# One TensorE step and one reciprocal for the denominators of a global and a 3x3 local softmax

## The chip, the cores and the metric

The kernel runs on one core of a Trainium2 chip, all in float32, in one launch. The metric is the device time of that launch in microseconds (us), the median of three executions.

## What is computed

The input is x, 4 images of 64x64 pixels with 256 channels. Two layers follow one another. Layer 0 is full self-attention over the 4096 pixels of an image. Layer 1 is a depthwise 3x3 convolution to 768 channels, a two-layer perceptron, and attention in a 3x3 window. Cut to what matters:

```
# layer 0
energy = einsum('bnd,bmd->bnm', q, k)                 # q, k: 32 channels
attn   = softmax(energy, axis=-1)                     # over 4096 pixels
x      = gamma * einsum('bnm,bmc->bnc', attn, v) + x
# layer 1
perceived = depthwise_conv3x3(x)                      # 3 outputs per channel
h  = x + w_up2 @ gelu(w_up1 @ perceived + b_up1) + b_up2
q, k, v = split(h @ w_qkv.T + b_qkv)
w  = softmax over the 9 neighbours of (q . k_neighbour / 16)
out = h + sum_i w_i * v_neighbour_i
```

So there are two softmaxes, and each needs a denominator per pixel: the sum of the exponentials.

## The kernel before

**Layout.** Channels or keys lie on the 128 partitions, pixels along the free axis. One *slot* is a block of 512 pixels (8 image rows); 4 images of 8 blocks make 32 slots, numbered 0 to 31. The kernel writes each engine's instruction order out by hand: the order of the Python calls is the order in which each engine runs its instructions.

**The global attention of one slot** walks over its 4096 keys in 16 *points* of 256 keys. `energy` (L262) makes 512 keys' scores with four matmuls of 32 rows each, in a tile `e` that takes four PSUM banks and has one buffer. `weight` (L274) is ScalarE's exponential from `e` into a tile `p` (three buffers, 256 keys each); it runs two points ahead of `product` (L279), which multiplies `p` with the values into the two accumulators `acc`. `add_up` (L293) adds the `p` tiles on VectorE into `den`, 128 partial sums per pixel, one on each partition.

**The denominators.** `finish` (L305), at the end of a slot, multiplies `den` with a 128x128 matrix of ones (`dps`, L310), which sums over the partitions and leaves the same sum on all 128; VectorE takes the reciprocal (`rden`, L312), scales the two accumulators (`o`, L316) and adds them to the image in SBUF (L320). The local attention does the same five slots behind (`LAG_ATT`): `local_sum` (L601, mostly GpSimd) makes `lsum`, again 128 partial sums per pixel, at point 12 of a slot, and `local_denominator` (L629), at point 1 of the next slot, multiplies it with ones (`ld`, L631) and takes a reciprocal (`lrden`, L633). `local_product` (L636) multiplies by it at points 3 and 5.

**The other work of a slot** is laid on the points by the list `jobs` (L701): `hidden` (L380, the perceptron's first layer, four parts of 6 matmuls, each followed by ScalarE's Gelu), `update` (second layer), `guide`, `scores`, `local_values`. Each takes a PSUM bank by `job_bank`; in the slots these and `dps` share two banks with the tag "m", taken in turn. After the last slot comes a *tail* (L774 on), in which the banks go round over "m", "e" and "acc", and VectorE still has much convolution (`perceive`, L366) to do.

**The next image.** During the last slot of an image (slots 7, 15 and 23; each of them is the slot with `nxt`, L711) the queries, keys and values of the next image's eight blocks are projected. `fetch` (L166) brings each block of x with two DMAs from the SyncE queue into a tile `xc` (two buffers). The first two, for the blocks 8 and 9 say, are issued ahead of point 0 (L714); `project_qk` (L195), which works on both blocks, follows at the end of point 1. A tile that takes over a buffer is written only when the last reader of the tile before it, in program order, is done, wherever in the program that reader stands.

Of the kernel before, what the change touches and what calls it, by code (L numbers as in the profile page):

```python
# [15 lines left out]
P = 128  # L16
# [3 lines left out]
CH = C // P  # L20
HP, WP = H + 2, W + 2
NB = 512
# [21 lines left out]
LAG_PERC, LAG_HID, LAG_ATT = 2, 3, 5  # L44
# [3 lines left out]
def attention_then_perception_kernel(  # L48
# [19 lines left out]
    nc = tc.nc  # L68
# [8 lines left out]
    ones = const.tile([P, P], F32, tag="ones", name="ones")  # L77
# [5 lines left out]
    def unshifted():  # L83
# [4 lines left out]
        def tile_of(shape, tag, name, bufs=1):  # L88
            return pool.tile(shape, F32, tag=tag, name=name, bufs=bufs)

        def bank(tag, name):
            return psum.tile([P, NB], F32, tag=tag, name=name, bufs=2)
# [5 lines left out]
        def job_bank(name):  # L98
            turns.append(turns.pop(0))
            if turns[-1] == "e":  # L100
                return psum.tile([P, GRP, NB], F32, tag="e", name=name, bufs=1)[:, 0, :]
            return bank(turns[-1], name)
# [7 lines left out]
        def renew(slot, cs=slice(0, CH)):  # L110
            b, g = divmod(slot, NBLK)
            at = slice((1 + g * RB) * WP, (1 + (g + 1) * RB) * WP)
            nc.sync.dma_start(out=xp[:, cs, at], in_=x[b, :, cs, at])
# [44 lines left out]
        def watch(values):  # L158

            nc.gpsimd.tensor_tensor(watched, watched, values, ALU.add)  # L160
# [85 lines left out]
        def projections(s):  # L246
            pair = [lambda: project_qk(s)] if s % 2 == 0 else []
            return pair + [lambda: project_v(s, 0), lambda: project_v(s, 1)]
# [8 lines left out]
                )  # L257


        energies, weights, sums, accs = {}, {}, {}, {}  # L260

        def energy(s, G):  # L262

# [41 lines left out]
        def finish(s):  # L305
            g = s % NBLK
            den = sums.pop(s)

            dps = bank("m", f"dps_{s}")
            nc.tensor.matmul(dps, lhsT=ones, rhs=den[:, 0, :], start=True, stop=True)  # L310
            rden = tile_of([P, NB], "rden", f"rden_{s}", 2)
            nc.vector.reciprocal(rden, dps)  # L312
            os = []
            for c, acc in enumerate(accs.pop(s)):
                o = tile_of([P, NB], "o", f"o_{s}_{c}", 3)
                nc.vector.scalar_tensor_tensor(o, acc, gam[:, 0:1], rden, ALU.mult, ALU.mult)  # L316
                os.append(o)
            for c, o in enumerate(os):
                dst = xv[:, c, 1 + g * RB : 1 + (g + 1) * RB, 1 : 1 + W]
                nc.vector.tensor_tensor(  # L320
                    dst, o.rearrange("p (h w) -> p h w", w=W), dst, ALU.add
                )
            watch(den[:, 0, :])
            watch(rden)
            for o in os:
                watch(o)


        percs, hids, hs = {}, {}, {}
# [95 lines left out]

        guides, lvs, near_ws, lsums, lrdens, pads, spares, results = [], {}, {}, {}, {}, {}, {}, {}
        wg = pool.tile([P, CH, C], F32, tag="wg", name="wg")
        small = pool.tile([P, 2 * CH + 1], F32, tag="small", name="small")  # L430
        bg, wc, bc = small[:, :CH], small[:, CH : 2 * CH], small[0:1, 2 * CH :]
# [194 lines left out]
            watch(t)  # L626
            lsums[s] = t

        def local_denominator(s):  # L629
            ps = job_bank(f"ld_{s}")  # L630
            nc.tensor.matmul(ps, lhsT=ones, rhs=lsums.pop(s), start=True, stop=True)  # L631
            lrdens[s] = tile_of([P, NB], "rden", f"lrden_{s}", 2)
            nc.vector.reciprocal(lrdens[s], ps)  # L633
            watch(lrdens[s])
# [26 lines left out]
        def job(f, s, *args, n=NSLOT):  # L661
            return [lambda: f(s, *args)] if 0 <= s < n else []
# [32 lines left out]
        for slot in range(NSLOT):  # L695
            b, g = divmod(slot, NBLK)
            if b > 0:
                renew(slot)
            k, a = slot - LAG_HID, slot - LAG_ATT

            jobs = [  # L701
                job(hidden, k, 0), job(hidden, k, 1) + job(local_denominator, a),
                job(hidden, k, 2), job(local_product, a, 0), job(hidden, k, 3),
                job(local_product, a, 1), job(update, k, 0), job(update, k, 1), [],
                job(guide, k, 0), job(guide, k, 1), job(scores, k, 0),
                job(scores, k, 1) + job(local_sum, k - 1), job(local_values, k, 0),
                job(local_values, k, 1), [],
            ]
            if slot in (1, 2):
                jobs[0] = [lambda: next(combine)] * 2  # L710
            nxt = []  # L711
            if g == NBLK - 1 and b + 1 < B:
                nxt = [projections(slot + 1 + i) for i in range(NBLK)]
                for i in range(2):  # L714
                    fetch(slot + 1 + i)
            if slot == 0:
                nxt = [early_jobs[2 * i : 2 * i + 2] for i in range(NG)]
            conv = perceive(slot - LAG_PERC, whole) if slot >= LAG_PERC else iter(())
            n_steps, stepped = NPC * (TAPS - 1), 0
            extra = iter(())  # L720
            if slot == NSLOT - 1:

                extra = perceive(slot - 1, [(i, 0, RB - 1) for i in range(NPC // 2)])
            for point in range(points):
                G, half = divmod(point, 2)
                after = slot + (G + 1) // NG, (G + 1) % NG
                if half == 0:
                    if G == NG // 2 and slot + 1 < NSLOT:
                        spread_queries(slot + 1)

                    if G == NG // 2:
                        for do in job(border, k - 1):
                            do()
                    if after[0] < NSLOT:
                        energy(*after)
                if after[0] < NSLOT:
                    weight(*after, half)
                for do in jobs[point]:
                    do()
                product(slot, G, half)  # L740

                if point == 0:
                    add_up(slot, 0, 0)
                if point < points - 1:
                    add_up(slot, *divmod(point + 1, 2))

                while stepped < min(n_steps, -(-(point + 1) * n_steps // (points - 2))):
                    next(conv, None)
                    stepped += 1
                    if stepped % 2:  # L750
                        next(extra, None)
                if slot == 0 and point == NG:

                    next(combine)
                    blqk = loaded(b_lqk, "blqk")
                    wperc = loaded(w_perc, "wperc")
                    bperc = loaded(b_perc, "bperc")
                    wup1 = loaded(w_up1, "wup1")
                    bup1 = loaded(b_up1, "bup1")
                    wup2 = loaded(w_up2, "wup2")  # L760
                    bup2 = loaded(b_up2, "bup2")
                    nc.sync.dma_start(out=wlv, in_=w_qkv[:, :, 2 * C :])
                    blv = loaded(b_lv.partition_broadcast(P), "blv", [P, C])
                if nxt and half == 1:
                    for do in nxt[G]:
                        do()
                    if slot and G + 2 < NBLK:
                        fetch(slot + 1 + G + 2)
            for _ in chain(conv, extra):
                pass  # L770
            finish(slot)


# [15 lines left out]
        last = NSLOT - 1  # L789
        for k in range(NSLOT - LAG_HID, NSLOT):  # L790
            a = k - LAG_ATT + LAG_HID
            if k == last:
                for _ in conv:
                    pass
            run(
                (hidden, k, 0, 6), (hidden, k, 1, 6), (local_denominator, a, 0),
                (hidden, k, 2, 6), (local_product, a, 0, 1), (hidden, k, 3, 6),
                (local_product, a, 1, 1), (update, k, 0, 3), (update, k, 1, 2),
                (local_values, k, 0, 1), (guide, k, 0, 1), (local_values, k, 1, 1),
                (guide, k, 1, 1),  # L800
            )
            if k == last:
                below(NSLOT)
                local_values(NSLOT, 0)
            run((scores, k, 0, 1), (scores, k, 1, 1), (border, k - 1, 0), (local_sum, k - 1, 0))
        guide(NSLOT, 0)
        run(
            (scores, NSLOT, 0, 0), (scores, NSLOT, 1, 0), (border, last, 0),
            (local_denominator, last - 1, 0), (local_sum, last, 0),
            (local_product, last - 1, 0, 0), (local_product, last - 1, 1, 0),  # L810
            (local_denominator, last, 0), (local_product, last, 0, 0), (local_product, last, 1, 0),
        )

        test = [tile_of([P, NB], "o", f"test_{i}", 3) for i in range(2)]
# [405 lines left out]
```

## Time and profile before

| | |
|---|---|
| time, median of 3 | 3648.2 us (3646.78 to 3649.05) |
| span of the profiled execution | 3645.1 us, 29412 instructions |
| TensorE (PE) busy | 3599.6 us, 99% |
| VectorE (DVE) busy | 2448.6 us, 67% |
| ScalarE (ACT) busy | 1176.8 us, 32% |
| GpSimd (POOL) busy | 721.2 us, 20% |
| mean granted TensorE clock | 0.996 of full |
| reciprocals, `rden` and `lrden` | 32 and 32, 107.4 us of VectorE each |

PE is TensorE's matmuls and PEld its weight loads; POOL is GpSimd. One float32 matmul of the program stands as two instructions in the profile, so 2048 products are 4096 records. Records of a run overlap a little: what a matmul takes of TensorE's time is read from the starts of neighbours, not from the duration beside it. In lists of groups, the number after `x` is a count, then come busy time and the mean of one in ns, and after the second bar the idle time of the engine just before the group with the releaser that ended it. In a timeline the columns are start, duration (us), engine, line, operation, count and, in brackets, the idle time before it.

### The profile page before, as it was taken

How to read it: one execution, taken by the hardware profiler on the slowest of the kernel's cores; microseconds unless marked ns; L12 is line 12 of the kernel's file. 1: busy time of each engine (PE TensorE's matmuls, PEld its weight loads, DVE VectorE, ACT ScalarE, POOL GpSimd, SP SyncE). 2: the span in 40 equal slices, each digit the busy share in tenths (PEclk: the TensorE clock that was granted, in tenths of full speed). 3: DMA queues.
4: the chain of work that ended last, by engine and by line, in shares of the span. 5: the costliest groups of instructions: out<-in, count | busy, mean ns of one | idle time of the engine just before them, and what ended most of it. 6: DMA issues, size and time to landing. Idle time of an engine off the chain costs nothing.

```text
span 3645.1 us, 29412 instructions
## 1 busy us (share of the span) xinstructions
PE 3599.6 (99%) x11350; PEld 1706.7 (47%) x11350; DVE 2448.6 (67%) x2727; ACT 1176.8 (32%) x1324; POOL 721.2 (20%) x725
## 2 busy tenths in 40 slices
PE   9999999999999999999999999999999999999987
PEld 4444444454444444455444444444544444444444
DVE  3385676657666767766677667676666776766884
ACT  2233333323333333332333333333333333333321
POOL 1010112111222221121112222211121122222232
PEclk9999999999999999999999999999999999999999
DMA  3000000010000000101000000011100000000000
GB/s 103 6 3 4 0 9 21 18 44 15 15 15 3 12 15 15 27 23 38 15 15 15 15 3 12 15 27 33 28 15 15 15 15 15 4 12 15 6 10 21
DMA packets 84532, 64.68 MB, mean 18 GB/s; under 512 B 57280, under 2 KB 62528, under 8 KB 84256
## 3 DMA queue, kind: packets, MB, share of 16 engines
q1 hardware_dynamic: 83568, 62.19, 6.3%
q8 instruction: 91, 1.49, 0.2%
q10 hardware_dynamic: 816, 0.53, 0.0%
q14 instruction: 57, 0.47, 0.0%
HBM read 41.52 MB, written 18.81 MB: 17 GB/s over the span
## 4 chain that ended last, share of the span: by engine, by line
PE 97%; DVE 2%; issue 0%; ACT 0%; POOL 0%; DMA 0%; SPq 0%; ACTq 0%; DVEq 0%; POOLq 0%
PE acc L287 49%; PE hid L385 18%; PE e L268 7%; PE dx L411 6%; PE lv L537 3%; PE g L496 3%; PE v L234 3%; PE s L573 2%; PE lo L642 2%; DVE perc L366 1%; PE qk L200 1%; PE ld L631 1%; PE dps L310 1%; DVE lrden L633 0%; DVE rden L312 0%; PE c L520 0%
## 5 line engine op out<-in xcount | busy, mean ns | idle before, releaser
L287 PE MATMUL acc<-p,v 128*128 128x512 f32 x4096 | 1842.2, 595 | 0.1
L366 DVE SCALAR_TENSOR_TENSOR perc<-xp,wperc,perc 128x512 f32<-128x512 f32 (+2 forms) x1560 | 1305.9, 840 | 314.7 <-ACT perc L362 280.7
L287 PEld LDWEIGHTS acc<-p,v 128*128 128x128 f32 x4096 | 769.4, 190 | 917.3 <-issue 913.5
L276 ACT ACTIVATE p<-e 128x1024 f32<-128x1024 f32 x512 | 524.4, 1024 | 1516.1 <-PE e L268 904.1
L385 PE MATMUL hid<-perc,wup 128*128 128x512 f32 x1536 | 689.2, 598 | 1.6 <-DVE perc L366 1.6
L301 DVE TENSOR_TENSOR den<-den,p 128x1024 f32<-128x1024 f32 x480 | 597.0, 1244 | 44.3 <-ACT p L276 40.6
L385 PEld LDWEIGHTS hid<-perc,wup 128*128 128x128 f32 x1536 | 284.2, 190 | 391.4 <-issue 384.3
L268 PE MATMUL e<-qa,ka 32*128 32x512 f32 x2048 | 292.0, 640 | 0.0
L160 POOL TENSOR_TENSOR watched<-watched,lo 128x512 f32<-128x512 f32 x64 | 130.4, 2037 | 624.4 <-DVE lo L649 624.1
L411 PE MATMUL dx<-hid,wup 128*128 128x512 f32 x512 | 232.8, 598 | 0.0
L389 ACT ACTIVATE hid<-hid,bup 128x512 f32<-128x512 f32 x128 | 88.0, 687 | 400.3 <-PE hid L385 400.3
L312 DVE RECIPROCAL rden<-dps 128x512 f32<-128x512 f32 x32 | 107.4, 3358 | 160.4 <-PE dps L310 160.4
L592 POOL TENSOR_TENSOR lp<-lp,near 128x396 f32<-128x396 f32 x60 | 58.1, 970 | 739.0 <-ACT lp L588 739.0
L276 ACT ACT_TABLE_LOAD x116 | 148.8, 1283 | 151.2 <-issue 120.1
L549 DVE TENSOR_TENSOR lv<-lv,blv 128x256 f32<-128x256 f32 x130 | 49.2, 420 | 193.2 <-PE lv L537 193.2
L633 DVE RECIPROCAL lrden<-ld 128x512 f32<-128x512 f32 x32 | 107.4, 3357 | 82.3 <-PE ld L631 82.3
L417 DVE SCALAR_TENSOR_TENSOR h<-dx,bup,xp 128x256 f32<-128x256 f32 x128 | 56.0, 480 | 152.1 <-PE dx L411 149.3
L268 PEld LDWEIGHTS e<-qa,ka 32*128 32x128 f32 x2048 | 79.9, 182 | 164.6 <-issue 162.0
L411 PEld LDWEIGHTS dx<-hid,wup 128*128 128x128 f32 x512 | 94.7, 190 | 129.2 <-issue 120.2
L362 ACT ACTIVATE perc<-xp,bperc,wperc 128x512 f32<-128x512 f32 (+2 forms) x195 | 154.6, 796 | 0.0
L389 ACT ACT_TABLE_LOAD x119 | 152.7, 1283 | 2.2
L537 PE MATMUL lv<-wlv,h 128*128 128x256 f32 x520 | 128.6, 390 | 12.3 <-DVE h L417 11.0
(91 smaller groups left out, 2030.9 us busy)
## 6 DMA issues: line engine op xcount, KB each, us to landing
xp<-in_x SPq DMA_DIRECT2D x30, 528.0 KB, 4.1
out<-lo SPq DMA_DIRECT2D x60, 256.0 KB, 2.0
xc<-in_x SPq DMA_DIRECT2D x48, 256.0 KB, 3.8
qa<-packed SPq DMA_DIRECT2D x124, 64.0 KB, 2.1
ka<-st SPq DMA_DIRECT2D x124, 16.0 KB, 1.8
packed<-st SPq DMA_DIRECT2D x31, 64.0 KB, 1.9
wup<-in_w_up SPq DMA_DIRECT2D x1, 1536.0 KB, 7.0
xp<-in_x SPq DMA_DIRECT2D x4, 264.0 KB, 3.9
```

Of the source, the lines that this page charges most:

```text
L160: nc.gpsimd.tensor_tensor(watched, watched, values, ALU.add)
L234: nc.tensor.matmul(ps[:, i * C : (i + 1) * C], lhsT=xc[:, kin, bass.ts(2 * pair + i, P)], rhs=wv[:, kin, :], start=(kin == 0), stop=(kin = ...
L268: nc.tensor.matmul(e[:, j, :], lhsT=key[rows, :], rhs=queries[s][rows, :], start=True, stop=True,)
L276: nc.scalar.activation(p, energies[s, G][:, 2 * half : 2 * half + 2, :], AF.Exp)
L287: nc.tensor.matmul(accs[s][c], lhsT=v[:, 2 * half + i, bass.ts(c, P)], rhs=p[:, i, :], start=(first and i == 0), stop=(G == NG - 1 and hal ...
L301: nc.vector.tensor_tensor(den, den, p, ALU.add)
L362: nc.scalar.activation(acc, win, AF.Identity, bias=bperc[:, half, j : j + 1], scale=wt)
L366: nc.vector.scalar_tensor_tensor(acc, win, wt, acc, ALU.mult, ALU.add)
L385: nc.tensor.matmul(ps, lhsT=wup1[:, i, bass.ts(d, P)], rhs=percs[s][i], start=(i == 0), stop=(i == NPC - 1),)
L389: nc.scalar.activation(hids[s][:, d, :], ps, AF.Gelu, bias=bup1[:, d : d + 1])
L411: nc.tensor.matmul(ps, lhsT=wup2[:, d, bass.ts(c, P)], rhs=hids[s][:, d, :], start=(d == 0), stop=(d == NHC - 1),)
L537: nc.tensor.matmul(ps[:, half * C : (half + 1) * C], lhsT=keys_of(s, t, half, kin), rhs=wlv[:, kin, :], start=(kin == 0), stop=(kin == CH ...
```

## The change

`finish` now sums both denominators at once. The matrix of ones is cut to 64 columns and used twice: once on `den`, with its result on PSUM partitions 0 to 63, and once on `lsum` of the local attention, with its result on partitions 64 to 127 of the same bank. The two matmuls sit on the two column halves of TensorE. One reciprocal then turns both. Since each result lies on one half only, copies bring it to both halves: two on VectorE for the global denominator, within `finish`, and two on ScalarE for the local one, in `local_denominator`, which keeps its place at point 1 of the next slot. The purpose is to save a matmul on TensorE and a reciprocal on VectorE in each slot.

It holds where both exist: in `finish` of slots 4 to 31, which is 28 times. Slots 0 to 3 keep the old form, and so do the last four local denominators, in the tail, under the name `last_denominator`. Three things come with it: the reciprocal goes to a tile `turned`, for which the two buffers `xc` are borrowed; the second part of `hidden` moves from point 1 to point 0, ahead of the slot's first `product`; and the tail calls `job_bank` one time fewer.

```diff
         def finish(s):
             den = sums.pop(s)
             dps = bank("m", f"dps_{s}")
-            nc.tensor.matmul(dps, lhsT=ones, rhs=den[:, 0, :], start=True, stop=True)
             rden = tile_of([P, NB], "rden", f"rden_{s}", 2)
-            nc.vector.reciprocal(rden, dps)
+            a = s - LAG_ATT + 1
+            if a < 0:
+                nc.tensor.matmul(dps, lhsT=ones, rhs=den[:, 0, :], start=True, stop=True)
+                nc.vector.reciprocal(rden, dps)
+            else:
+                for half, weights_ in zip(halves, (den[:, 0, :], lsums.pop(a))):
+                    nc.tensor.matmul(
+                        dps[half], lhsT=ones[:, : P // 2], rhs=weights_, start=True, stop=True
+                    )
+                turned = tile_of([P, CH, NB], "xc", f"turned_{s}", 2)[:, 0, :]
+                nc.vector.reciprocal(turned, dps)
+                for half in halves:
+                    nc.vector.tensor_copy(rden[half], turned[halves[0]])
+                lrdens[a] = turned
...
+        def local_denominator(s):
+            turned, lrdens[s] = lrdens[s], tile_of([P, NB], "rden", f"lrden_{s}", 2)
+            for half in halves:
+                nc.scalar.copy(lrdens[s][half], turned[halves[1]])
+            watch(lrdens[s])
...
-        def local_denominator(s):
+        def last_denominator(s):
...
-                job(hidden, k, 0), job(hidden, k, 1) + job(local_denominator, a),
+                job(hidden, k, 0) + job(hidden, k, 1), job(local_denominator, a),
...
-                (hidden, k, 0, 6), (hidden, k, 1, 6), (local_denominator, a, 0),
+                (hidden, k, 0, 6), (hidden, k, 1, 6),
+                (local_denominator if k < last - 1 else last_denominator, a, 0),
```

More of the change, by code (lines that the diff above doesn't have):

```diff
@@ L257, in spread_queries @@
                 )
-        energies, weights, sums, accs = {}, {}, {}, {}
+        energies, weights, sums, accs, lsums, lrdens = {}, {}, {}, {}, {}, {}
+        halves = slice(0, P // 2), slice(P // 2, P)
         def energy(s, G):
@@ L423, in update @@
                 )
-        guides, lvs, near_ws, lsums, lrdens, pads, spares, results = [], {}, {}, {}, {}, {}, {}, {}
+        guides, lvs, near_ws, pads, spares, results = [], {}, {}, {}, {}, {}
         wg = pool.tile([P, CH, C], F32, tag="wg", name="wg")
@@ L808, in unshifted @@
             (scores, NSLOT, 0, 0), (scores, NSLOT, 1, 0), (border, last, 0),
-            (local_denominator, last - 1, 0), (local_sum, last, 0),
+            (last_denominator, last - 1, 0), (local_sum, last, 0),
             (local_product, last - 1, 0, 0), (local_product, last - 1, 1, 0),
-            (local_denominator, last, 0), (local_product, last, 0, 0), (local_product, last, 1, 0),
+            (last_denominator, last, 0), (local_product, last, 0, 0), (local_product, last, 1, 0),
         )
```

## The prediction

> **What bounds the kernel now.** I read the chain of work that ended last first, because it says whose time is the kernel's time. Its shares by engine:
>
> ```profile
> PE 97%; DVE 2%; issue 0%; ACT 0%; POOL 0%; DMA 0%; SPq 0%; ACTq 0%; DVEq 0%; POOLq 0%
> ```
>
> Then the list of waits, for TensorE alone (total us, times, longest):
>
> ```profile
> PE lv L537 <- DVE h L417: 11.0, 3, 6.6
> PE good_sum L822 <- DVE good L820: 6.5, 1, 6.5
> PE v L234 <- DMA wv<-in_w_v: 5.5, 1, 5.5
> PE ld L631 <- POOL lsum L625: 5.1, 1, 5.1
> ```
>
> These and all smaller waits lie in the first slots or in the tail; between 800 and 2400 us the list for TensorE is empty. So inside the slots a microsecond taken from TensorE's queue is a microsecond of the kernel, one in which it is made to wait is lost, and VectorE's, ScalarE's and GpSimd's work costs nothing unless TensorE comes to wait for it. Third, the timeline where slot 22 ends and slot 23 begins, one of the three slots that fetch the next image; only TensorE's matmuls are shown:
>
> ```profile
> 2465.88 1.02 PE L310 MATMUL dps<-den,ones 128*128 128x512 f32 x2
> 2466.83 1.14 PE L268 MATMUL e<-qa,ka 32*128 32x512 f32 x8
> 2467.90 5.42 PE L385 MATMUL hid<-perc,wup 128*128 128x512 f32 x12
> 2473.16 3.60 PE L287 MATMUL acc<-p,v 128*128 128x512 f32 x8
> 2476.59 5.31 PE L385 MATMUL hid<-perc,wup 128*128 128x512 f32 x12
> 2481.74 1.02 PE L631 MATMUL ld<-lsum,ones 128*128 128x512 f32 x2
> 2482.60 3.60 PE L287 MATMUL acc<-p,v 128*128 128x512 f32 x8
> 2486.12 1.94 PE L200 MATMUL qk<-xc,wqk 128*64 128x512 f32 x8
> 2487.99 3.72 PE L234 MATMUL v<-wv,xc 128*128 128x256 f32 x16
> ```
>
> From the starts: `dps` holds TensorE 0.95 us (2465.88 to 2466.83), `ld` 0.86, a `hidden` part 5.15 to 5.26, a `product` 3.43. The row of `qk` is the nearest to the new operation: four matmuls of 64 columns, two on each half, in 1.87 us, where four full ones would take 4 x 0.86 = 3.44.
>
> **What the skill says.** The Trainium skill, "TensorE: Matmul & The Clock Gate", Part 3: Packing small matmuls, says that matmuls on different tiles of the array run at the same time; the `qk` row agrees, 1.87 us against 3.44. "TensorEngine Tiling (Array Packing)", Key Properties: changing the tiling mode drains the engine. The trace agrees, with about 0.09 us: `dps`, followed by the four-row mode of `e`, takes 0.95 where `ld`, followed by its own mode, takes 0.86. "Perfetto Trace Analysis", DMA Instruction — HWDGE: the issuing sequencer sits in the semaphore wait before it starts the DMA, so a waiting DMA holds those behind it. In the rows of before I see no such long wait; it is the point of the change's third part.
>
> **The change part by part.**
>
> *TensorE, saved.* Before, each pair costs 0.95 + 0.86 = 1.81 us. After: two passes side by side, 2 x 0.43 = 0.86, plus what `qk` shows over the bare streaming, 1.87 - 4 x 0.43 = 0.15, plus one drain to enter the mode, 0.09: 1.10. Bounds: 0.95 (no extra) and 1.96 (one half after the other, 4 x 0.43 + 0.24). I take 1.10, since `qk` has the same shape, so 0.71 a slot. Of the 28 pairs, 27 lie in slots (the last is in the tail): 27 x 0.71 = **19.2 us saved**.
>
> *VectorE.* A reciprocal less, 3.36 us, and two 64x512 copies more. The nearest row is the copy into `xc`, 128x512 at 446 ns, so 0.9 for both. Inside a slot neither counts: `rden` is needed by `o`, which frees `acc` for the next `product`. From the start of the step that is 1.10 + 0.1 + 3.36 + 0.9 + 1.4 = 6.9 us, while TensorE gets to that product only after `e` and now two `hidden` parts, 1.10 + 1.07 + 2 x 5.26 = 12.7. The bank of `dps` comes free at 4.6; the second `hidden`, which takes it, starts at 7.4. `lsum` must be there by the end of the slot: one slot earlier GpSimd ends it at 2345.7, 13 us ahead of `dps` at 2358.6.
>
> *The moved `hidden`.* Same matmuls, same modes: 0. But point 1 loses its filler. The exponential of point 1 (`p` has three buffers) waits for the first `product`, and the `e` of point 2 waits for that exponential. The row of the same pattern, point 3 of slot 22:
>
> ```profile
> 2385.21 3.60 PE L287 MATMUL acc<-p,v 128*128 128x512 f32 x8
> 2388.88 1.28 ACT L276 ACT_TABLE_LOAD   x1 [2.08 <-issue]
> 2390.17 1.02 ACT L276 ACTIVATE p<-e 128x1024 f32<-128x1024 f32 x1
> ```
>
> It ends 5.98 us after that `product` starts. TensorE gets to the next `e` after two products, 6.86. It fits with 0.9 us to spare, so 0. ScalarE's two copies stand behind this exponential; the work that hides them is the second product and the `e` of point 2.
>
> *The borrowed `xc`.* This is a new wait on the path. `turned_6` is read by ScalarE's copies at point 1 of slot 7, but `fetch(9)`, ahead of point 0 of slot 7, takes its buffer (4, 5, 6 then 8, 9 in turn over two buffers). So that DMA, first issued at the slot's start, now waits for the copies, and SyncE's queue with it. Likewise in slots 15 and 23. Counted from the start of the slot's first product: exponential done 5.98, two copies of 512 elements at 616 ns (the row of ScalarE's copy into `xc`) 7.2, DMA issued about 7.4. The landing of these DMAs:
>
> ```profile
> DMA to landing us min/median/max: 3.0/3.8/6.2
> ```
>
> The first half lands at 11.2, the second, issued 0.55 later, at 11.75, and the last `qk` pair, 0.95 us, then ends at about 12.8. Without a wait `qk` would end at 6.86 + 1.87 = 8.7. TensorE stands **4.1 us**, three times: **12.3 us lost** (3.3 to 6.5 each by the bounds of the landing, so 10 to 20). All that waits behind `qk` in TensorE's queue is delayed with it, and nothing gives it back, as TensorE has no idle time later in these slots.
>
> *The tail.* Here VectorE is the bound from the last `dps` on:
>
> ```profile
> 3474.25 13.02 DVE L366 SCALAR_TENSOR_TENSOR perc<-xp,wperc,perc 128x64 f32<-128x64 f32 x30
> 3487.18 3.35 DVE L633 RECIPROCAL lrden<-ld 128x512 f32<-128x512 f32 x1
> 3490.45 5.36 DVE L366 SCALAR_TENSOR_TENSOR perc<-xp,wperc,perc 128x512 f32<-128x512 f32 x6
> ...
> 3505.23 1.19 PE L537 MATMUL lv<-wlv,h 128*128 128x256 f32 x2 [6.65 <-DVE h L417]
> ```
>
> VectorE has no gap between them, and TensorE stands 6.65 us for it. The reciprocal at 3487 goes (-3.36), two copies come (+0.9), and the joint step ends 0.24 later than `dps` alone: **2.2 us saved**. The turn of banks shifts by one; going through it I find each bank read out before its next use, so 0.
>
> *Sum:* -19.2 - 2.2 + 12.3 = -9.1; 3648.2 - 9.1 = **3639.1 us**.
>
> **The rivals.**
> 1. *The late DMA is hidden*: the buffer is free earlier than I read, or the data come in time. For it: the queue has nothing else to do then. Against: point 1 has now only 3.43 us of TensorE work between the exponential's release and `qk`. It gives 3648.2 - 21.4 = 3626.8.
> 2. *A new wait in every slot at the `e` of point 2*: the margin of 0.9 us is the thinnest in the plan; a convolution start (0.80 us on ScalarE) or a late VectorE sum before the exponential would use it up. At 0.5 us in 27 slots, +13.5: 3652.6, slower by 0.12%, which counts as no change. Against it: the copy of `den` that frees `p` ends 11 us after `dps` starts, 5 us before it is needed.
> 3. *The halves don't overlap*, or the step waits between them. Each pair then costs 1.96, 0.15 more than before: +4.1 + 12.3 - 2.2 = +14.2, so 3662.4, slower. Against it: the `qk` row.
>
> **How the numbers follow.** My forecast 62%, rival 1 15%, rival 2 13%, rival 3 and other ways to be slower 10%. Within my forecast the landing and the pair's cost spread the time over about 3634 to 3646. The range runs from rival 1 to the upper end of mine: 3626 to 3646; that leaves out rival 3, most of rival 2 and a little of the rest, some 2 in 10. The bound of 0.2% lies at 3640.9 and 3655.5. Faster: rival 1 and about three quarters of mine, 0.62. Same: the rest of mine and most of rival 2, 0.26. Slower: 0.12.
>
> **What would show it.** In slots 8 to 14 the joint step should hold TensorE for about 1.1 us, and no wait of TensorE should appear. The list of waits should have a new entry, `qk` waiting for the DMA into `xc`, three times, about 4 us each. If it is missing, rival 1 holds; if `e` waits for `p` in many slots, rival 2; if the step takes near 2 us, rival 3. The reciprocals should be 36 in all with half their time gone and the end unmoved by it but for the tail. The prediction is wrong if TensorE waits in ordinary slots, or if the three waits are under 2 us or over 7.

## The result, and the profile after

| | before | after |
|---|---|---|
| time, median of 4 | 3648.62 us (3646.78 to 3649.54) | 3633.94 us (3631.02 to 3635.74) |
| span of the profiled execution | 3645.1 us | 3629.3 us |
| TensorE busy | 3599.6 us | 3584.8 us |
| VectorE busy | 2448.6 us | 2379.1 us |
| ScalarE busy | 1176.8 us | 1136.1 us |

The change makes the kernel 14.7 us faster, a ratio of 0.996 with a 95% interval of 0.9942 to 0.9977. The chain of work that ended last is still TensorE's, with 97% of the span as before.

The list of TensorE's waits after the change (total us, times, longest) has one entry that before had not, `qk` waiting for a DMA, and the tail's waits are shorter:

```profile
PE lv L558 <- DVE h L438: 9.7, 3, 5.3
...
PE good_sum L844 <- DVE good L842: 5.2, 1, 5.2
PE qk L200 <- DMA xc<-in_x: 3.6, 3, 1.2
PE ld L652 <- POOL lsum L646: 3.2, 1, 3.2
```

The timeline of TensorE at the same place as before, the end of slot 22 and the beginning of slot 23 (start, duration, engine, line, operation):

```profile
2448.07 7.03 PE L288 MATMUL acc<-p,v 128*128 128x512 f32 x16
2455.03 0.64 PE L320 MATMUL dps<-den,ones 128*64 128x512 f32 x1
2455.04 0.64 PE L320 MATMUL dps<-lsum,ones 128*64 128x512 f32 x1
2455.51 0.59 PE L320 MATMUL dps<-den,ones 128*64 128x512 f32 x1
2455.52 0.59 PE L320 MATMUL dps<-lsum,ones 128*64 128x512 f32 x1
2456.04 1.14 PE L269 MATMUL e<-qa,ka 32*128 32x512 f32 x8
2457.11 10.57 PE L406 MATMUL hid<-perc,wup 128*128 128x512 f32 x24
2467.51 7.03 PE L288 MATMUL acc<-p,v 128*128 128x512 f32 x16
2474.47 1.07 PE L200 MATMUL qk<-xc,wqk 128*64 128x512 f32 x2
2476.73 2.04 PE L200 MATMUL qk<-xc,wqk 128*64 128x512 f32 x6 [1.18 <-DMA xc<-in_x]
2478.69 3.72 PE L234 MATMUL v<-wv,xc 128*128 128x256 f32 x16
```

Three things are to be seen. The four passes of the joint step start in pairs, 0.01 us apart, so the halves run side by side. The step holds TensorE from 2454.94 (2448.07 and 16 passes of 0.43) to 2456.04: 1.10 us, where `dps` and `ld` took 1.81. And `qk` stops after its first pair: from 2474.38 (two products after 2467.51) to `v` at 2478.69 it takes 4.31 us, where before it took 1.96 counted in the same way. The list shows only 1.2 us of wait for these 2.35 us, because it counts the time in which TensorE stood idle. The starts of the single passes show the rest. Before, the eight passes of `qk` start in four pairs, the two halves side by side. After, the first matmul runs alone (passes at 2474.47 and 2474.95), two run as pairs when the data are there (2476.73 and 2477.21), and the last runs alone again (2477.69 and 2478.17).

Since the step stands once in each slot, its start is a ruler. I laid the starts of before and after side by side:

| slot | `dps` starts, before | after | difference | change from the slot ahead |
|---|---|---|---|---|
| 4 | 462.88 | 459.96 | -2.92 | |
| 5 | 570.12 | 566.49 | -3.63 | -0.71 |
| 6 | 677.36 | 673.02 | -4.34 | -0.71 |
| 7 | 820.48 | 817.85 | -2.63 | +1.71 |
| 8 | 927.72 | 924.38 | -3.34 | -0.71 |
| 14 | 1571.62 | 1564.03 | -7.59 | -0.71 |
| 15 | 1714.74 | 1708.84 | -5.90 | +1.69 |
| 23 | 2609.01 | 2599.80 | -9.21 | +1.64 |
| 31 | 3466.11 | 3451.24 | -14.87 | -0.71 |

Each ordinary slot is 0.71 us shorter; slots 7, 15 and 23 are 1.6 to 1.7 longer, so about 2.4 us are lost in each (2.41, 2.40 and 2.35 from the unrounded starts), 7.2 in all. From slot 4 to slot 31 that is -27 x 0.71 + 7.2, or -11.95 by the table. The remaining 3.85 of the 15.8 us between the two spans lie ahead of slot 4 (2.92) and in the tail (0.93).

The part ahead of slot 4 is not the change's. Slot 1's step already starts 3.01 us earlier (184.29 before, 181.28 after), and up to there no instruction differs; the first joint step, in slot 4, then starts 0.09 later behind its product. In the stretch from 110 to 130 us, the granted TensorE clock (third number from the end) of the kernel before is

```profile
110.00:130.00 20.00, 18.08 (x55) 7.55 (x54) 12.81 (x12) 4.10 (x4) 4.54 (x3) 0.91 0.00 0
```

and that of the kernel after

```profile
110.00:130.00 20.00, 18.08 (x59) 7.63 (x58) 13.74 (x12) 3.84 (x4) 4.54 (x3) 1.00 0.00 0
```

In the other profiles of this study it is 0.91 or 1.00 without regard to the kernel: the first experiment below has 0.91 and begins slot 1's step at 184.06 us, the second has 1.00 and begins it at 181.12, though the two run the same instructions up to there. So some 3 us at the start vary from execution to execution, and the difference of two spans is to be read without them.

### The profile page after: what moved, and what is told of

The parts are those of the page before. It is cut to its first block, busy times and chain, and to the rows that moved or that the text cites. A ratio compares the mean times of both kernels' runs of the same rounds, so it can differ in the third digit from the quotient of the medians.

```text
span 3629.3 us, 29422 instructions
## 1 busy us (share of the span) xinstructions
PE 3584.8 (99%) x11350; PEld 1694.0 (47%) x11350; DVE 2379.1 (66%) x2755; ACT 1136.1 (31%) x1322; POOL 707.8 (20%) x725
## 4 chain that ended last, share of the span: by engine, by line
PE 97%; DVE 2%; DMA 0%; ACT 0%; issue 0%; POOL 0%; SPq 0%; ACTq 0%; POOLq 0%; DVEq 0%
PE acc L288 49%; PE hid L406 18%; PE e L269 7%; PE dx L432 6%; PE lv L558 3%; PE g L517 3%; PE v L234 3%; PE s L594 2%; PE lo L663 2%; PE qk L200 1%; DVE perc L387 1%; PE dps L320 1%; DVE lrden L654 0%; PE c L541 0%; DMA xc<-in_x 0%
## 5 line engine op out<-in xcount | busy, mean ns | idle before, releaser
L324 DVE RECIPROCAL turned<-dps 128x512 f32<-128x512 f32 x28 | 94.0, 3358 | 133.1 <-PE dps L320 133.1
L239 DVE TENSOR_TENSOR v<-v,bv 128x512 f32<-128x512 f32 x64 | 44.2, 691 | 138.8 <-PE v L234 138.4
L663 PEld LDWEIGHTS lo<-lp,lv 128*128 128x128 f32 x768 | 114.0, 197 | 30.8 <-issue 30.5
```

Source lines behind the costliest of these rows:

```text
L663: nc.tensor.matmul(pv[:, rows, columns(half)], lhsT=lvs[block, t, half][:, bass.ts(c, P)], rhs=near_ws[block, half][:, t, of, :], start=(i ...
```

## The experiments

The ratios are against the kernel before; slots are compared with the profile of the kernel after the change. Two theories were on the table. *Mine*: inside the slots only TensorE's time counts, the gain is the overlap of the halves, and the three stands of `qk` come from ScalarE's copies holding a buffer of `xc`. *The rival*: VectorE's relief, or the new order, makes the gain, or the stands have another cause.

### Another buffer for the reciprocal

```diff
-                turned = tile_of([P, CH, NB], "xc", f"turned_{s}", 2)[:, 0, :]
+                turned = tile_of([P, NB], "st", f"turned_{s}")
```

> The reciprocal's result goes to the single buffer of st instead of the two of xc; all else as after the change. Theory A (the 2.35 us that qk stands in slots 7, 15 and 23 come from xc's buffer being read by ScalarE's copies at point 1): the three waits of qk for the DMA are gone, each of these slots is 2.4 us shorter, in all -7.1, so about 3627. Rival (the stand is the price of having only 7 us of TensorE work between the first product and qk, whichever buffer is used, or it comes back at the reciprocal, which must now wait for the DMAs that read st): no change, 3634.

Measured: 3625.61 us, ratio 0.994 (0.9926 to 0.9953). Slots 7, 15 and 23 are shorter than after the change by 2.41, 2.40 and 2.35 us, all other slots from slot 3 on agree within 0.01, and the wait of `qk` for the DMA is gone from the list. `st` is written again by ScalarE only after the copies, in ScalarE's own order, and no reciprocal waits for its readers, the DMAs: the idle time ahead of the 28 reciprocals is 133.3 us in all, and 133.1 after the change, all of it put down to `dps`. So the borrowed `xc` cost 7.2 us, and it was avoidable.

### The copies earlier

```diff
-                job(hidden, k, 0) + job(hidden, k, 1), job(local_denominator, a),
+                job(hidden, k, 0) + job(hidden, k, 1) + job(local_denominator, a), [],
```

> The two ScalarE copies of the local denominator move from point 1 to the end of point 0, behind the second Gelu and ahead of the exponential; xc stays borrowed. Theory A: the DMA is issued some 6 us sooner after the second hidden part, lands before TensorE comes to qk, and the three waits are gone, -7.1, about 3627; the exponential still ends in time, so no wait in other slots. Rival (the DMA waits for something else than the copies): qk still waits 1.2 us, 3634.

Measured: 3625.53 us, ratio 0.9941 (0.9928 to 0.9955). The same three slots are shorter by the same 2.41, 2.40 and 2.35 us. In the timeline of this run ScalarE's copies, the DMA from SyncE's queue (SPq) and `qk` of slot 23 are

```profile
2463.46 1.24 ACT L346 COPY lrden<-turned 64x512 f32<-64x512 f32 x2
2464.73 0.99 SPq L189 DMA_DIRECT2D xc<-in_x  x2
2469.51 1.94 PE L200 MATMUL qk<-xc,wqk 128*64 128x512 f32 x8
```

The DMA starts within 0.03 us of the copies' end (2464.70), and `qk` finds its data. After the change the same DMA was issued at 2473.46, 0.02 us after its copies ended at 2473.44. The DMA follows the copies wherever they are put: they are what it waits for.

### Two reciprocals

```diff
-                nc.vector.reciprocal(turned, dps)
+                for half in halves:
+                    nc.vector.reciprocal(turned[half], dps[half])
```

> One reciprocal for each half of dps instead of one for both: VectorE gets back the 3.36 us a slot that the change took from it, TensorE's work is as after the change. Theory A (inside the slots only TensorE's time counts): slots 8 to 14 keep their period, the tail grows by 2 to 3.4 us, so 3636 to 3637. Rival B (the slots became shorter because VectorE was relieved): the 0.71 us a slot are lost again, 27 x 0.71 = 19 us, so about 3653.

Measured: 3656.44 us, ratio 1.0026 (1.0015 to 1.0036), slower than before the change. My number was wrong, and the rival's nearly right: each slot is 0.72 us longer than after the change. The list of waits names a new one for TensorE:

```profile
PE hid L407 <- DVE turned L325: 12.2, 27, 0.5
```

and the timeline of slot 10's beginning shows one of the 27:

```profile
1034.55 0.64 PE L320 MATMUL dps<-den,ones 128*64 128x512 f32 x1
1035.70 6.74 DVE L325 RECIPROCAL turned<-dps 64x512 f32<-64x512 f32 x2 [5.30 <-PE dps L320]
1036.63 5.42 PE L407 MATMUL hid<-perc,wup 128*128 128x512 f32 x12
1042.51 5.42 PE L407 MATMUL hid<-perc,wup 128*128 128x512 f32 x12 [0.46 <-DVE turned L325]
```

The second part of `hidden` waits for a reciprocal whose result it doesn't use. What it needs is the bank: the tag "m" has two, `dps` took one and the first part of `hidden` the other. The reciprocals end at 1042.44, and TensorE goes on at 1042.51. Counted by starts, the first part holds TensorE for 5.88 us (1036.63 to 1042.51) instead of 5.15, which is the slot's loss; the 0.46 in brackets counts from a modelled end. I had the two times for one reciprocal in the prediction, 4.6 against 7.4 us, and had not added 3.36 to the first. That the loss has almost the size of the gain is chance, and the run alone doesn't decide between the bank and VectorE's load.

### A spare reciprocal that doesn't hold the bank

```diff
                 nc.vector.reciprocal(turned, dps)
+                nc.vector.reciprocal(rden, turned)
```

> After the change, with a second, superfluous reciprocal on VectorE between the first and the copies; it reads turned in SBUF and not dps, and its result is overwritten. VectorE's load in finish is that of the run with two reciprocals, but the PSUM bank of dps is free after the first. Theory A' (in the run with two reciprocals TensorE lost 0.72 us a slot because the second part of hidden takes the bank of dps, and that bank was held until 7.9 us after the step began, while TensorE came to it at 7.4): slots 8 to 14 have the period of after the change, 106.53 us, and no wait of hidden; only the tail grows, by some 3.5 us, so about 3637. Rival B (VectorE's load itself sets the slots): 0.7 us a slot lost again, about 3656.

Measured: 3636.75 us, ratio 0.9969 (0.9958 to 0.9979). VectorE does the same amount of work ahead of `o` as with two reciprocals, but the second reads SBUF. The wait of `hidden` is gone from the list, and the slots have the period of after the change within 0.01 us (slot 8 begins its step at 924.37, slot 14 at 1564.02; after the change 924.38 and 1564.03). Slot 10's beginning, where both parts of `hidden` run through:

```profile
1032.05 3.36 DVE L324 RECIPROCAL turned<-dps 128x512 f32<-128x512 f32 x1 [5.30 <-PE dps L320]
1032.98 10.57 PE L407 MATMUL hid<-perc,wup 128*128 128x512 f32 x24
1035.44 3.35 DVE L325 RECIPROCAL rden<-turned 128x512 f32<-128x512 f32 x1
```

The tail, counted from the last step to the end of the span, grows from 178.04 to 183.23 us. TensorE's longest wait there goes from 5.28 to 8.7, which is the one reciprocal more. Of the remaining 1.8, 0.3 is lost ahead of the next `lv` and 1.5 behind TensorE's last matmul; why is open. So 3.36 us more of VectorE a slot cost nothing in the slots as long as they hold no bank, and the loss of the run above was the bank.

### The halves one after the other

```diff
-                for half, weights_ in zip(halves, (den[:, 0, :], lsums.pop(a))):
-                    nc.tensor.matmul(
-                        dps[half], lhsT=ones[:, : P // 2], rhs=weights_, start=True, stop=True
-                    )
+                nc.tensor.matmul(
+                    dps[halves[0]], lhsT=ones[:, : P // 2], rhs=den[:, 0, :], start=True, stop=True
+                )
...
+                if point == points - 1 and slot >= LAG_ATT - 1:
+                    sum_local(slot)
                 product(slot, G, half)
```

`sum_local`, not shown, takes the bank of `dps` and makes the half on `lsum` in its partitions 64 to 127.

> The two 64-column matmuls are kept, but the local one is moved ahead of the slot's last product, so they can't run side by side. Theory A (the gain is the overlap of the two halves): each then takes about 0.86 + 0.18 us of TensorE, 2.1 together instead of 1.1, so +1.0 us in 27 slots, about 3661, slower than before the change. Rival (a 64-column matmul is cheaper by itself, or the gain has another source): no change, 3634.

Measured: 3672.2 us, ratio 1.0065 (1.0051 to 1.0079). Each ordinary slot is 1.19 us longer than after the change. From the timeline:

```profile
1035.16 3.60 PE L288 MATMUL acc<-p,v 128*128 128x512 f32 x8
1038.68 1.07 PE L346 MATMUL dps<-lsum,ones 128*64 128x512 f32 x2
1039.69 3.70 PE L288 MATMUL acc<-p,v 128*128 128x512 f32 x8
1043.32 1.07 PE L319 MATMUL dps<-den,ones 128*64 128x512 f32 x2
1044.32 1.14 PE L269 MATMUL e<-qa,ka 32*128 32x512 f32 x8
```

A half alone holds TensorE 1.10 us (the product before it ends its passes at 1038.59, the next begins at 1039.69) and 1.20 (1043.12 to 1044.32), as much as both together or more. Without the overlap the two matmuls cost 2.30, more than the 1.81 of the two full ones, and the gain is gone. The run also adds a second change of the tiling mode and doesn't price the two apart. With one change only, four passes in a row would take 1.96 by the prediction's estimate, which is still no gain. My number, 3661, was too low: I had put the halves at 2.1 instead of 2.30, which makes 5 of the 11 us. In slots 7, 15 and 23 `v` waits besides, 0.8 us each, for VectorE to read out a bank; the rest was not followed up.

### The second part of hidden back at point 1

```diff
-                job(hidden, k, 0) + job(hidden, k, 1), job(local_denominator, a),
+                job(hidden, k, 0), job(local_denominator, a) + job(hidden, k, 1),
```

> After the change, with the second part of hidden back at point 1, behind the copies of the local denominator in the program; xc stays borrowed. Theory A (the DMA into xc shows because the move left point 1 with 6.9 us between the first product and qk): with 5.2 us more of TensorE's work there the DMA lands in time, the three waits are gone, -7.1, about 3626, and the other slots keep 106.53 us, since the first product is still reached (7.4 us after the step begins) later than o frees its bank (6.2). Rival (the move is needed for the slots' gain): the slots grow, over 3634.

Measured: 3627.23 us, ratio 0.9944 (0.993 to 0.9957). The three slots are shorter than after the change by 2.41, 2.40 and 2.35 us again, and the other slots equal within 0.01 from slot 3 on. Here the DMA is issued at 2467.35, 4.9 us ahead of `qk` at 2472.24. So the stand needed both: the borrowed buffer, and the move that took 5.2 us of TensorE's work from between the exponential and `qk`. In this run the part stands behind ScalarE's copies; with it ahead of them, the order of before the change, the borrowed buffer was not run.

### The move alone

```diff
-                job(hidden, k, 0), job(hidden, k, 1) + job(local_denominator, a),
+                job(hidden, k, 0) + job(hidden, k, 1), job(local_denominator, a),
```

> The kernel before, with only the second part of hidden moved from point 1 to point 0. Theory A (the move gives nothing by itself): slots keep 107.24 us, time as before, 3648. Rival (the fewer reloads of ScalarE's tables or the new order give part of the gain): faster by some us.

Measured: 3646.92 us, ratio 0.9999 (0.9991 to 1.0007). From slot 3 to slot 31 each slot equals that of before within 0.01 us. The move saves ScalarE table loads, 87 ahead of its exponentials in this run where before there were 116 (87 after the change too), and they are worth nothing here.

Of the versions tried, those with another buffer, with the copies early and with `hidden` back all beat the kernel after the change by the same 7.2 us of the slots; their medians, 3625.5 to 3627.2, lie closer together than the runs of one of them (3623.3 to 3627.4).

## Why the prediction was right, point by point

- **TensorE's saving: right.** The `qk` row gave 1.10 us for the joint step and 0.71 a slot; measured 1.10 and 0.71. The parts of the sum fit too: the first pass starts 0.09 us behind the product's end (2454.94 to 2455.03), and the passes take 1.01, 0.15 over 0.86. The run with the halves apart shows that the gain hangs on the overlap.
- **VectorE costs nothing inside the slots: right in the change, with a margin I had not priced.** The spare reciprocal shows that the load is hidden, the two reciprocals that the bank of `dps` is a near limit: it comes free 2.8 us before TensorE takes it by my working, and a second reciprocal on it is already too much. The two copies took 420 ns each, near the 446 of the copy into `xc` from which I estimated them. The reciprocals are 36 in all, as forecast, with 120.8 us instead of 214.8.
- **The moved `hidden`: no cost in ordinary slots, as said**, shown by the move alone and by the run with the part back. The margin that I called the thinnest was wider than I thought; see the next point.
- **The borrowed `xc`: mechanism right, size off.** This is the mis-sized term: 12.3 us predicted, 7.2 measured. The step that failed is "exponential done 5.98". I took it from the row of point 3. There the table load starts only when the product is over: 8 passes from 2385.21 end at 2388.65, the load begins at 2388.88. At point 1 it starts earlier. The timeline of ScalarE in slot 23 of the kernel after:

```profile
2468.30 0.80 ACT L383 ACTIVATE perc<-xp,bperc,wperc 128x512 f32<-128x512 f32 x1
2469.12 1.28 ACT L277 ACT_TABLE_LOAD   x1
2471.15 1.02 ACT L277 ACTIVATE p<-e 128x1024 f32<-128x1024 f32 x1 [0.75 <-PE acc L288]
2472.20 1.24 ACT L346 COPY lrden<-turned 64x512 f32<-64x512 f32 x2
```

  The load is over at 2470.40, while the first product still runs; only the exponential waits for it. It ends 4.66 us after that product began (2467.51), 1.3 earlier than I said. The kernel before shows the same at point 1, in the timeline that I had read for TensorE:

```profile
2475.85 1.28 ACT L276 ACT_TABLE_LOAD   x1 [1.10 <-DVE den L298]
2477.14 1.02 ACT L276 ACTIVATE p<-e 128x1024 f32<-128x1024 f32 x1
```

  The load is released by VectorE's `den`, not by the product, and the exponential ends 5.00 us after that product began (2473.16). I used the row of another point though that of the right one was there. Most of the rest is the landing: the matmul that waited for the DMA starts 3.27 us after the issue (2473.46 to 2476.73), where I took the median of 3.8. Two smaller things were wrong. By my own figures the last `qk` pair ends at 12.7 and not 12.8, so the sum should have been 12.0. And long waits of SyncE's queue were there before: its own list has one of 154.0 us, for `lo`. New after the change are the three for ScalarE's copies, 13.0 us each; behind them stood only the DMAs from `st`, which come after `qk` in any case.

  I had named waits of `qk` under 2 us as a sign that I was wrong. By the list they are 1.2 us each, so by that sign the forecast fails. The sign was badly put: the time lost in each slot, which is what the sum needs, is 2.4, and the list doesn't hold what `qk` lost when its halves no longer ran side by side.
- **The tail: right in kind, a little less.** 2.2 us were predicted. Counted from the end of the last product, `lv` begins 37.24 us later instead of 39.12, so 1.9 us are saved; TensorE's longest wait falls from 6.65 to 5.28. VectorE's row in the tail of the kernel after has no reciprocal between the convolution steps:

```profile
3460.36 18.60 DVE L387 SCALAR_TENSOR_TENSOR perc<-xp,wperc,perc 128x64 f32<-128x64 f32 x36
3478.88 0.68 DVE L670 TENSOR_TENSOR lo<-lo,lrden 128x512 f32<-128x512 f32 x1
...
3488.39 1.19 PE L558 MATMUL lv<-wlv,h 128*128 128x256 f32 x2 [5.28 <-DVE h L438]
```

  The profiled span keeps only 0.93 of it, and the profile before was quick at its very end. Over the last 30 us its granted clock was 0.78, after the change 0.61, and 24 matmul records of `lo` took 3.26 us there and 5.24 after. The run with the move alone has the same tail as before the change, and in it the clock was 0.61, these records took 5.33, and the tail 180.57 us from the last step on, against 178.95 before and 178.04 after.
- **The sum.** -9.1 us predicted, -14.7 measured. Of the difference of 5.6, the mis-sized stand is 5.1; the tail's 0.3 goes the other way, and the rest, 0.8, is within the spread of single runs, 4.7 us for the kernel after.
- **The rivals.** The late DMA was not hidden, but 2.4 of the expected 4.1 us were left, for the reasons above; no new wait appeared at the `e` of point 2; the halves do overlap.

## What to carry to other kernels

Where one engine bounds a kernel, count the change in that engine's queue from the starts of neighbouring instructions, and then look for what the change borrows: a buffer taken over from another use brings that use's next writer into the chain, and a bank held longer can stop a matmul that never reads it. Price a wait from the row of the very place it will stand at, since two instructions of one line can carry different waits. Splitting a matmul into column halves paid here only when both halves were issued together, and a half whose partner is late loses more than the wait that the list shows.

## What the runs showed of the hardware

- A single 64-column float32 matmul of 512 columns among full-width ones held TensorE for 1.10 to 1.20 us, where a full-width one takes 0.86 among its own kind; two of them on the two halves together took 1.10. The Trainium skill, "TensorEngine Tiling (Array Packing)", Key Properties, says that a change of the tiling mode drains the engine. These runs agree: 0.24 to 0.34 us stand over the 0.86, which is an estimate of what going into the mode and out of it cost here, if nothing else is in it.
- Half the partitions took as long as all: a VectorE reciprocal of 64x512 took 3.356 us, of 128x512 3.358; the one of 128x512 took as long from SBUF (3.35) as from PSUM (3.36). ScalarE's copy of 64x512 took 616 ns, as that of 128x512 before.
